# A four-layer graph network: the order of the attention's matmuls at the ends of a block, and the queues of the first loads

## Chip, cores and metric

The kernel runs on one core of a Trainium2 chip. The metric is the device time of one execution in microseconds. A core has these engines: PE (TensorE, matmuls), DVE (VectorE), ACT (ScalarE), POOL (GpSimd) and SP (SyncE, here only issuing transfers). Each works through its own queue of instructions in order; transfers are carried by 16 DMA engines.

## What is computed

x is 4096 x 256 in f32, adj a 4096 x 4096 matrix of 0 and 1 (about one entry in 128 is 1). Four layers follow one another; each takes h = relu(layernorm(x)) and adds its output to x. The change is in the attention of layers 0 and 2, cut to what matters:

```python
# layer 0 (h: 4096 x 256); its gating, which follows, is left out here
Wh = h @ W
e = Wh @ a_src + (Wh @ a_dst).T
e = jnp.where(e > 0, e, 0.2 * e)
e = jnp.where(adj > 0, e, jnp.float32(-9000000000000000.0))
h_attn = jax.nn.softmax(e, axis=1) @ Wh
...
# layer 2
h = x @ W
e = (h @ a[:D, 0])[:, None] + (h @ a[D:, 0])[None, :]
e = jnp.where(e > 0, e, 0.01 * e)
att_logits = jnp.where(adj > 0, e, -1e12)
return jax.nn.elu(jax.nn.softmax(att_logits, axis=1) @ h)
```

Layer 1 is a mean over neighbours, layer 3 an attention with queries and keys.

## The kernel before

**Stages.** By the trace, layer 0's projection and first loads take the first 76 us, its attention lasts to about 625 us, its dense part to 1230, layer 1 to 1530, layer 2's attention from there to 2018, layer 3 to the end.

**Attention in blocks.** `class Attention` (L192) serves layers 0 and 2. The 4096 rows are 32 tiles of 128. A block is a group of row tiles: in layer 0 two blocks of 2 tiles and seven of 4 (`cuts`, L453), in layer 2 eight of 4. For each block the columns are gone through in 16 pairs of column tiles (c, c + 1). In `run` (L338) a pair goes through four steps:

- `logits` (L325): DVE forms the logits of the pair in a buffer y (L332, one instruction for each of the two column tiles), POOL subtracts the mask from y (L336). There are 8 y buffers; a buffer is free again when the matmuls have read it.
- ACT takes the exponential of y (L363, two instructions).
- PE adds the pair to the block's accumulators (L374): for each row tile r one accumulator of 128 x 257 in PSUM, its first column the row sums of the exponentials. A pair of a block with 4 row tiles is 8 matmuls; in the trace an f32 matmul is two instructions, so 16.
- At a block's last pair, DVE inverts the row sums (`rden`, L382), and a finish function scales the accumulators out of PSUM: in layer 0 `finish0` (L442), even r on ACT (L449), odd r on DVE (L447), into xs; in layer 2 `finish2` (L920), even r on ACT (L930), odd on DVE (L926), into hp, with an exponential on ACT (L934) and two additions on DVE (L936, L937) behind it.

The program text runs the logits three pairs ahead of the matmuls (`LAG`). Layer 0 has 4 accumulator buffers (`att.run(es, LEAD, 4, ahead)`, L654), layer 2 has 5 (L1119). In the kernel before, the matmuls of a pair are written column tile by column tile, and for each over all r:

```python
for k in range(2):
    for r, acc in enumerate(accs[b]):
        nc.tensor.matmul(
            out=acc, lhsT=y[:, r, k, :], rhs=self.v[:, c + k, 0 : D + 1],
            start=(c + k == 0), stop=(c + k == NT - 1),
        )
```

**The maxima of the next block.** While a block is worked on, `reach` (L265) builds the running minimum for the next one on DVE (L278 for the first column tile, L280 for the others). At its end `top` (L286) copies it (ACT L291), transposes it (PE L294), reduces it (DVE L297 to L302) and transposes the result (PE, abT, L304), from which the rows for the next block's logits are spread over the partitions (PE L313 or two DMAs, L319 and L320).

**The mask.** In layer 0 `ahead` (L515) loads one adjacency tile after another (POOL's DMA, L486), transposes it on PE in 8 instructions (cT, L495), turns it into the mask on ACT (`turned`, L500) and stores it (codesT, SP, L520). Layer 2 loads the masks again with SP's DMAs.

**The beginning.** `load(1)` (L608) issues the first adjacency tile on POOL. SP then issues the eight DMAs of x, 512 KB each, and W, a_src and a_dst (`weights`, L219) between the first and second of them. `block0(b)` takes one x block at a time, staggered: statistics on DVE (L122, L123), the mean taken off on ACT, DVE and POOL (L629, L633), the power for the deviation on POOL (L117), for b = 0 the products of W with a_src and a_dst on DVE (`columns`, L242), further loads `load(2 * b + 6)` on POOL, the transposed masks of one unit, then transposes (L145) and the projection on PE (L154) with ACT's copies (L256), and two steps of `reach`.

**What sets the order.** The program text is written for all engines at once; a scheduler orders the instructions of each engine's queue from it and adds the waits. An engine does not overtake within its queue.

Of the kernel before, what the change touches and what calls it, by code (L numbers as in the profile page):

```python
# [41 lines left out]
def kernel(ctx: ExitStack, tc: tile.TileContext, w: dict, out: bass.AP):  # L42
    nc = tc.nc
    x, adj = w["x"], w["adj"]
    N, D = x.shape
    NT = N // P
# [64 lines left out]
    def rstd_of(pool, mv, n, tag, rs=None):  # L111

        ve = pool.tile([P, n], F32, tag=f"{tag}_ve", name=f"{tag}_ve")
        nc.vector.tensor_scalar(ve, mv[:, :, 1], EPS, None, ALU.add)
        if rs is None:
            rs = pool.tile([P, n], F32, tag=f"{tag}_rs", name=f"{tag}_rs")
        nc.gpsimd.tensor_tensor(rs, ve, mhalf[:, :n], ALU.pow)  # L117
        return rs

    def stats_of(pool, src, mv, tag):  # L120
        st = pool.tile([P, 6], F32, tag=f"{tag}_st", name=f"{tag}_st")
        nc.vector.bn_stats(st, src)  # L122
        nc.vector.bn_aggr(mv, st)  # L123
# [68 lines left out]
    class Attention:  # L192
# [145 lines left out]
        def run(self, es, lead, n_acc, ahead=lambda n: None):  # L338

            self.y_p = es.enter_context(tc.tile_pool(name=f"{self.tag}_y", bufs=self.n_y))  # L340
            self.ps_b = es.enter_context(
                tc.tile_pool(name=f"{self.tag}_b", bufs=1, space=PSUM)
            )
            ps_acc = es.enter_context(
                tc.tile_pool(name=f"{self.tag}_acc", bufs=n_acc, space=PSUM)
            )
            pairs = [(b, c) for b in range(len(self.blocks)) for c in range(0, NT, 2)]
            LAG = self.lag
            ys, accs = {}, {}
            for n in range(len(pairs) + LAG):  # L350
                if n < len(pairs):
                    b, c = pairs[n]
                    ahead(n)
                    if n + PPB + lead < len(pairs):
                        self.reach(n + PPB + lead)
                    y = self.y_p.tile([P, RB, 2, P], F32, tag="y", name="y")
                    ys[n] = y = y[:, 0 : self.blocks[b]["n"], :, :]
                    self.logits(y, b, c, self.turned(b, c // QT))
                if n >= LAG:
                    b, c = pairs[n - LAG]  # L360
                    y = ys.pop(n - LAG)
                    for k in range(2):
                        nc.scalar.activation(  # L363
                            y[:, :, k, :], y[:, :, k, :], AF.Exp,
                            bias=self.sdst[:, c + k : c + k + 1],
                        )
                    if c == 0:
                        accs[b] = [
                            ps_acc.tile([P, D + 1], F32, tag="acc", name="acc")
                            for _ in range(self.blocks[b]["n"])  # L370
                        ]
                    for k in range(2):
                        for r, acc in enumerate(accs[b]):
                            nc.tensor.matmul(  # L374
                                out=acc, lhsT=y[:, r, k, :], rhs=self.v[:, c + k, 0 : D + 1],
                                start=(c + k == 0), stop=(c + k == NT - 1),
                            )
                    if c == NT - 2:
                        done = accs.pop(b)
                        rden = self.small.tile([P, RB], F32, tag="rden", name="rden")  # L380
                        for r, acc in enumerate(done):
                            nc.vector.reciprocal(rden[:, r : r + 1], acc[:, 0:1])  # L382
                        self.finish(self.blocks[b]["at"], done, rden)
# [46 lines left out]
    with ExitStack() as l0:  # L430
# [10 lines left out]
        with ExitStack() as es:  # L441
# [19 lines left out]
            att = Attention(es, "l0", 0.2, 3, 8, cuts, turned_of, finish0, ps_c)  # L461
# [19 lines left out]
            def load(up_to):  # L481
                for b, q, r in units[len(raw) : up_to]:
                    pool = first_p if len(raw) < FIRST else adj_p

                    raw.append(pool.tile([P, QW], BF16, tag="adj", name="adj_t"))
                    nc.gpsimd.dma_start(out=raw[-1], in_=adj[ts(b * RB + r, P), ts(q, QW)])  # L486

            def fresh(up_to):

                load(up_to)  # L490
                for g in range(made[0], up_to):
                    (b, q, r), a = units[g], raw[g]
                    ps = ps_c.tile([P, QW], BF16, tag="top", name="cT")
                    for i in range(QT):
                        nc.tensor.transpose(ps[:, ts(i, P)], a[:, ts(i, P)], identb)  # L495
                    if (b, q) not in turned:
                        pool = kept_p if (b * NQ + q) % 8 < KEPT else turned_p
                        turned[b, q] = pool.tile([P, RB, QT, P], BF16, tag="turned", name="turned")
                    ct = turned[b, q][:, r, :, :]
                    nc.scalar.activation(  # L500
                        ct.rearrange("p c i -> p (c i)"), ps, AF.Exp,
                        scale=math.log(UNIT / WIDE), bias=log_wide,
                    )
                made[0] = max(made[0], up_to)
# [95 lines left out]
            with ExitStack() as ps_:  # L600
                wp = ps_.enter_context(tc.tile_pool(name="l0_w0", bufs=1))
                work = ps_.enter_context(tc.tile_pool(name="l0_prep", bufs=2))
                small = ps_.enter_context(tc.tile_pool(name="l0_ps", bufs=4))
                pst = ps_.enter_context(tc.tile_pool(name="l0_pst", bufs=2, space=PSUM))
                psm = ps_.enter_context(tc.tile_pool(name="l0_psm", bufs=3, space=PSUM))
                first_p = ps_.enter_context(tc.tile_pool(name="l0_first", bufs=FIRST))

                load(1)  # L608
                for b in range(NB):
                    nc.sync.dma_start(  # L610
                        out=xs[:, ts(b, BT), :],
                        in_=x[ts(b, BW), :].rearrange("(t p) d -> p t d", p=P),
                    )
                    if b == 0:
                        att.weights(
                            wp, w["L0_gnn_W"], (w["L0_gnn_a_src"], w["L0_gnn_a_dst"]), nc.sync
                        )

                def block0(b):
                    xb = xs[:, ts(b, BT), :]  # L620
                    mv = small.tile([P, BT, 2], F32, tag="pl_mv", name="pl_mv")
                    for i in range(BT):
                        stats_of(small, xb[:, i, :], mv[:, i, :], "pl")


                    for i in range(BT):
                        mean = mv[:, i, 0:1]
                        if i == 0:
                            nc.scalar.activation(  # L629
                                xb[:, i, :], xb[:, i, :], AF.Identity, scale=-1.0, bias=mean  # L630
                            )
                        else:
                            (nc.gpsimd if i == BT - 1 else nc.vector).tensor_scalar(  # L633
                                xb[:, i, :], xb[:, i, :], mean, -1.0, ALU.subtract, ALU.mult
                            )
                    rs = rstd_of(small, mv, BT, "pl")
                    if b == 0:
                        att.columns(work)
                    load(2 * b + 6)
                    fresh(b + 1)  # L640
                    yield
                    hT = transposed_block(work, pst, xb, "hT", turned=True)
                    yield
                    att.project(b, hT, psm, rs)
                    yield
                    for n in range(2 * b, 2 * b + 2):
                        att.reach(n)

                run_staggered([block0(b) for b in range(NB)], 2)
                fresh(needed(PPB + FRESH - 1))  # L650
                for n in range(PPB, PPB + LEAD):
                    att.reach(n)
# [5 lines left out]
        wp = l0.enter_context(tc.tile_pool(name="l0_w", bufs=1))  # L658
# [467 lines left out]
    with ExitStack() as l3:  # L1126
# [4 lines left out]
        with ExitStack() as es:  # L1131
            wp = es.enter_context(tc.tile_pool(name="l3_w", bufs=1))
# [222 lines left out]
```

## Time and profile before

| what | value |
|---|---|
| median of 3 runs | 2989.58 us (2987.57 to 2996.24) |
| the profiled execution | 2990.5 us |
| span of its profile | 2988.7 us |
| mean granted PE clock in it | 0.989 |
| PE busy | 2866.0 us, 96% |
| DVE, ACT, POOL busy | 64%, 43%, 32% |

The span runs from the first to the last instruction of the profiled execution; the 1.8 us between it and that execution's time lie around it. The profile names each group of instructions by line and engine, with busy time, and, apart from it, the idle time just before its instructions with what ended that idle time. "DMA turned<-codesT" as the ending event is the landing of a mask tile loaded again. PEld is the load of the stationary operand, which runs beside PE.

### The profile page before, as it was taken

The numbers are of one execution on the slowest core, as the hardware profiler recorded it, in microseconds if no ns is written. First come the engines' busy times: TensorE is split into PE (matmuls) and PEld (weight loads), VectorE is DVE, ScalarE is ACT, GpSimd is POOL, SyncE is SP. The second block draws the span as 40 slices with busy tenths as digits, with TensorE's granted clock in tenths as the row PEclk, the third lists the DMA queues.
The fourth block names the chain that finished last, engine by engine and source line by source line (L and its number), as shares of the span: only waits on it lengthen the run. The fifth ranks groups of instructions, "written<-read, shape, count | busy, mean of one in ns | idle before, by whom it ended". The sixth has DMA issues, their size and how long they took to land.

```text
span 2988.7 us, 35212 instructions
## 1 busy us (share of the span) xinstructions
PE 2866.0 (96%) x13381; PEld 2335.5 (78%) x13381; DVE 1907.1 (64%) x3458; ACT 1279.1 (43%) x1963; POOL 947.8 (32%) x718
## 2 busy tenths in 40 slices
PE   7989999999999999899989999999999999999999
PEld 5778888866556665788878777888888888888888
DVE  5777777534555554477689888646766566566653
ACT  5666655459997323892264433433212112111211
POOL 4667665544444433220045555540000000000000
PEclk9999999999999999999999999999999999999999
DMA  5766665234553000595342122002111111111100
GB/s 131 201 146 145 128 139 133 71 58 70 80 79 65 8 8 8 136 248 164 113 170 87 68 78 78 29 11 68 58 51 47 37 34 62 39 34 62 34 8 8
DMA packets 109161, 238.62 MB, mean 80 GB/s; under 512 B 10736, under 2 KB 31200, under 8 KB 100288
## 3 DMA queue, kind: packets, MB, share of 16 engines
q1 hardware_dynamic: 71296, 167.26, 16.3%
q0 software_dynamic: 37696, 69.11, 14.9%
q8 instruction: 105, 1.72, 0.2%
q14 instruction: 64, 0.52, 0.1%
HBM read 265.63 MB, written 37.81 MB: 102 GB/s over the span
## 4 chain that ended last, share of the span: by engine, by line
PE 66%; ACT 9%; DVE 8%; issue 6%; POOL 6%; DMA 4%; SPq 0%; POOLq 0%; DVEq 0%; ACTq 0%
PE acc L374 18%; PE acc L1287 15%; PE s L154 15%; PE mm L154 8%; PE acc L1019 8%; POOL y L336 4%; ACT sign L180 4%; DVE y L332 2%; DVE run L280 2%; DMA turned<-codesT 1%; PE cT L495 1%; DMA a<-in_adj_dram 1%; PE q_ps L154 1%; ACT t L712 1%; DMA xs<-in_x_dram 1%
## 5 line engine op out<-in xcount | busy, mean ns | idle before, releaser
L374 PE MATMUL acc<-v,y 128*128 128x257 f32 x4096 | 930.8, 386 | 23.9 <-ACT hp L930 12.7
L374 PEld LDWEIGHTS acc<-v,y 128*128 128x128 f32 x4096 | 776.2, 192 | 137.0 <-ACT hp L930 17.0
L336 POOL TENSOR_TENSOR y<-y,turned 128x1024 f32<-128x1024 f32 (+1 forms) x272 | 545.3, 2015 | 320.2 <-DVE y L332 260.1
L363 ACT ACTIVATE y<-y,sdst 128x512 f32<-128x512 f32 (+1 forms) x544 | 350.5, 690 | 410.9 <-POOL y L336 410.7
L332 DVE SCALAR_TENSOR_TENSOR y<-ab_row,cdst,b 128x512 f32<-128x512 f32 (+1 forms) x544 | 371.0, 710 | 139.9 <-PE acc L374 124.1
L1287 PE MATMUL acc<-v,y 128*128 128x257 f32 x2048 | 454.5, 380 | 0.4 <-DVE rden L1295 0.4
L154 PE MATMUL s<-qT,hT 128*128 128x256 f32 x2048 | 445.2, 379 | 0.7 <-ACT qT L1235 0.7
L1280 ACT ACTIVATE y<-y 128x1024 f32<-128x1024 f32 x128 | 132.2, 1055 | 714.3 <-DVE y L1279 710.0
L154 PEld LDWEIGHTS s<-qT,hT 128*128 128x128 f32 x2048 | 389.0, 190 | 54.2 <-ACT qT L1235 1.4
L1287 PEld LDWEIGHTS acc<-v,y 128*128 128x128 f32 x2048 | 387.1, 190 | 55.9 <-issue 0.8
L180 ACT ACTIVATE sign<-a,limits 128x1024 bf16<-128x1024 bf16 x256 | 293.8, 1148 | 18.5 <-DMA a<-in_adj_dram 13.0
L1249 DVE SCALAR_TENSOR_TENSOR y<-code,s 128x512 f32<-128x512 bf16 x256 | 175.8, 687 | 100.7 <-PE s L154 100.5
L280 DVE SCALAR_TENSOR_TENSOR run<-turned,v,run 128x512 f32<-128x512 bf16 (+1 forms) x279 | 193.2, 692 | 31.8 <-ACT turned L500 22.7
L280 DVE SCALAR_TENSOR_TENSOR run<-turned,dst,run 128x512 f32<-128x512 bf16 x248 | 186.5, 752 | 24.5 <-DMA turned<-codesT 20.4
L1279 DVE TENSOR_TENSOR y<-y,top 128x1024 f32<-128x1024 f32 x128 | 146.2, 1215 | 43.0 <-PE top L1273 43.0
L1256 DVE TENSOR_TENSOR mx<-mx,y 128x512 f32<-128x512 f32 x224 | 154.8, 691 | 7.5
L500 ACT ACTIVATE turned<-cT,log_wide 128x1024 bf16<-128x1024 bf16 x128 | 139.2, 1105 | 29.9 <-PE cT L495 29.5
L173 POOL DMA_DIRECT2D a<-in_adj_dram x128 | 75.1, 588 | 198.4 <-ACT sign L180 144.8
L154 PE MATMUL mm<-kept 128*128 128x512 f32 x288 | 135.5, 610 | 2.4 <-ACT sz L807 1.4
L1019 PE MATMUL acc<-early,eq 128*128 128x512 f32 x512 | 128.8, 401 | 2.2 <-DVE early L421 1.9
L1019 PE MATMUL acc<-late,eq 128*128 128x512 f32 x512 | 122.6, 391 | 0.0
L1019 PEld LDWEIGHTS acc<-early,eq 128*128 128x128 f32 x512 | 97.0, 191 | 26.2 <-DVE early L421 2.1
(233 smaller groups left out, 3007.1 us busy)
## 6 DMA issues: line engine op xcount, KB each, us to landing
turned<-codesT SPq DMA_DIRECT2D x36, 1024.0 KB, 4.8
adj_t<-in_adj_dram POOLq DMA_DIRECT2D x128, 256.0 KB, 5.5
codesT<-turned SPq DMA_DIRECT2D x32, 1024.0 KB, 5.1
a<-in_adj_dram POOLq DMA_DIRECT2D x128, 256.0 KB, 4.7
code<-codesT SPq DMA_DIRECT2D x128, 256.0 KB, 5.5
code<-codesT SPq DMA_DIRECT2D x64, 512.0 KB, 8.1
ab_row<-l_ab_d SPq DMA_DIRECT2D x14, 512.0 KB, 5.6
xs<-in_x_dram SPq DMA_DIRECT2D x8, 512.0 KB, 12.5
```

What stands on the lines that cost most here:

```text
L154: nc.tensor.matmul(out=ps, lhsT=lhsT_of(k), rhs=rhs_of(k), start=(k == 0), stop=(k == n - 1))
L180: nc.scalar.activation(sign, self.came[g], AF.Sign, bias=limits[:, v : v + 1], accum_out=over[:, t, v, q : q + 1],)
L280: nc.vector.scalar_tensor_tensor(st["run"], code, dst, st["run"], ALU.subtract, ALU.min)
L332: nc.vector.scalar_tensor_tensor(y[:, :, k, :], st["ab"][:, 0, :, :], self.cdst[:, c + k : c + k + 1], st["b"], ALU.add, ALU.max,)
L336: nc.gpsimd.tensor_tensor(y, y, mask[:, :, c % QT : c % QT + 2, :], ALU.subtract)
L363: nc.scalar.activation(y[:, :, k, :], y[:, :, k, :], AF.Exp, bias=self.sdst[:, c + k : c + k + 1],)
L374: nc.tensor.matmul(out=acc, lhsT=y[:, r, k, :], rhs=self.v[:, c + k, 0 : D + 1], start=(c + k == 0), stop=(c + k == NT - 1),)
L1019: nc.tensor.matmul(out=acc, lhsT=eqs[c // (NT // 2)][:, ts(c % (NT // 2), P)], rhs=v1[c // BT][:, c % BT, :, :], start=(c == 0), stop=(c = ...
L1249: nc.vector.scalar_tensor_tensor(y[:, :, c : c + 2, :], st["code"][:, :, c : c + 2, :], -BIG / UNIT, ps, ALU.mult, ALU.add,)
L1256: nc.vector.tensor_tensor(mx, mx, y[:, :, c : c + 2, :], ALU.max)
L1279: nc.vector.tensor_tensor(part, part, top, ALU.subtract)
L1287: nc.tensor.matmul(out=accs[r], lhsT=st["y"][:, r, c, :], rhs=v3[:, c, :], start=(c == 0), stop=(c == NT - 1),)
```

## The change

It has two parts.

In `run`, the pairs of a block that are its last two, and in every block but the first its first two, are held back one at a time: when the second of the two is there, the matmuls of both are issued together, for r = 0 the four column tiles, then for r = 1, and so on. For all other pairs the order stays as it was. The number of matmuls, the buffers and the finish functions are unchanged. A y buffer is read to the end when the last row tile of its group has been added.

At the program's beginning the second adjacency tile is issued together with the first (`load(2)`), and W, a_src and a_dst are issued on ACT's queue before x's loop. SP issues x alone.

```diff
-            ys, accs = {}, {}
+            accs, held = {}, []
+            ys = {}
...
-                    for k in range(2):
-                        for r, acc in enumerate(accs[b]):
-                            nc.tensor.matmul(
-                                out=acc, lhsT=y[:, r, k, :], rhs=self.v[:, c + k, 0 : D + 1],
-                                start=(c + k == 0), stop=(c + k == NT - 1),
-                            )
+
+
+                    held.append((c, y))
+                    edge = NT - 2 - c < 4 or b > 0 and c < 4
+                    if edge and len(held) < 2:
+                        continue
+                    terms = [(r, c1 + k, y1) for r in range(len(accs[b]))
+                             for c1, y1 in held for k in range(2)]
+                    if not edge:
+                        terms.sort(key=lambda term: term[1])
+                    for r, j, y1 in terms:
+                        nc.tensor.matmul(
+                            out=accs[b][r], lhsT=y1[:, r, j % 2, :], rhs=self.v[:, j, 0 : D + 1],
+                            start=(j == 0), stop=(j == NT - 1),
+                        )
+                    held.clear()
                     if c == NT - 2:
...
-                load(1)
+                load(2)
+                att.weights(
+                    wp, w["L0_gnn_W"], (w["L0_gnn_a_src"], w["L0_gnn_a_dst"]), nc.scalar
+                )
                 for b in range(NB):
                     nc.sync.dma_start(
                         out=xs[:, ts(b, BT), :],
                         in_=x[ts(b, BW), :].rearrange("(t p) d -> p t d", p=P),
                     )
-                    if b == 0:
-                        att.weights(
-                            wp, w["L0_gnn_W"], (w["L0_gnn_a_src"], w["L0_gnn_a_dst"]), nc.sync
-                        )
```

## The prediction

> **What bounds the kernel now.** I read the page first: the engines' busy shares and the costliest groups (line, engine, operation; busy us, mean ns; idle time just before them and what ended most of it).
>
> ```profile
> PE 2866.0 (96%) x13381; PEld 2335.5 (78%) x13381; DVE 1907.1 (64%) x3458; ACT 1279.1 (43%) x1963; POOL 947.8 (32%) x718
> ...
> L374 PE MATMUL acc<-v,y 128*128 128x257 f32 x4096 | 930.8, 386 | 23.9 <-ACT hp L930 12.7
> ...
> L332 DVE SCALAR_TENSOR_TENSOR y<-ab_row,cdst,b 128x512 f32<-128x512 f32 (+1 forms) x544 | 371.0, 710 | 139.9 <-PE acc L374 124.1
> ```
>
> TensorE is the bound, and DVE waits 124.1 us for it (a y buffer comes free when the matmuls have read it). So only TensorE's own idle or slow time counts, and the attention's matmuls have 23.9 us of it. The waits of TensorE in layer 0's attention (172 to 625 us), then in layer 2 (1530 to 2018 us; total, times, longest):
>
> ```profile
> PE acc L374 <- ACT xs L449: 9.3, 6, 3.4
> PE abT L304 <- DVE ab L302: 7.8, 6, 1.4
> ```
> ```profile
> PE abT L304 <- DVE ab L302: 13.1, 7, 3.0
> PE acc L374 <- ACT hp L930: 12.7, 10, 3.0
> PE acc L374 <- issue: 1.9, 1, 1.9
> ```
>
> 9.3 + 12.7 = 22.0 us are waits for an accumulator to be emptied; the 1.9 is layer 2's first matmul, no block's end. One end of a block in the timeline (start, us, instruction, [idle before]):
>
> ```profile
> 1771.15 0.75 DVE L278 TENSOR_SCALAR run<-turned,dst 128x512 f32<-128x512 bf16 x1 [3.81 <-DMA turned<-codesT]
> ...
> 1775.37 0.16 DVE L382 RECIPROCAL rden<-acc 128x1 f32<-128x1 f32 x1
> 1775.57 0.57 ACT L930 ACTIVATE hp<-acc,minus,rden 128x256 f32<-128x256 f32 x1 [4.17 <-DVE rden L382]
> ...
> 1776.18 0.70 PE L374 MATMUL acc<-v,y 128*128 128x257 f32 x2 [2.99 <-ACT hp L930]
> ...
> 1777.75 0.55 ACT L930 ACTIVATE hp<-acc,minus,rden 128x256 f32<-128x256 f32 x1
> ```
>
> TensorE stops at 1773.2; DVE, late after a transfer, comes to the reciprocal at 1775.37; ACT empties r0 and TensorE starts. The clock beside such stalls (us; busy and instructions; granted clock; DMA share; GB/s):
>
> ```profile
> 508.70:512.10 3.40, 3.40 (x9) 0.51 0.30 118
> 512.10:515.50 3.40, 3.40 (x23) 1.00 1.00 318
> 1778.40:1781.80 3.40, 3.40 (x8) 0.50 0.00 0
> 1839.80:1846.60 6.80, 5.57 (x12) 0.50 0.08 10
> ```
>
> After three of the largest stalls (3.35 us ending at 508.44; 2.99 and 1.46 ending at 1776.18 and 1778.35; 2.57 ending at 1840.09) TensorE runs at half clock. The program's beginning, in the chain of waits (start, us, what):
>
> ```profile
> 9.53 24.00 DMA xs<-in_x_dram
> 33.55 0.43 DVE pl_st L122
> ```
>
> **What the Trainium skill says.** *Perfetto Trace Analysis*, "Matmuls": independent matmul groups should rotate through PSUM banks, so that emptying one overlaps the next group's matmuls. The trace shows what happens without enough overlap: 22.0 us. *TensorE: Matmul & The Clock Gate*, "What's actually happening": the clock halves after an idle window of about 3.4 us, and the windows run free of the kernel. Slow stretches of 3.40 and 6.80 us agree; that stalls of 2.57 to 3.35 us are enough is this trace's. *PSUM — Partial Sum Buffer*, "Engine vs sequencer instructions": queues of ScalarE, VectorE and GpSimd are strict FIFO; the reciprocal behind DVE's L278 agrees. *DMA: Bandwidth & Descriptors*, "Issuing engines are not separate DMA queues": transfers from all issuers interleave on the same 16 engines, only issue time is saved. Before the change x beside the adjacency tiles agrees: DVE takes up three successive x blocks of 0.52 MB at 20.46, 27.40 and 33.55 us, some 0.08 MB/us of x.
>
> **The sum, part by part.** *Grouped matmuls.* No instruction is added or removed: 4096 matmul instructions stay, two per matmul. In the timeline 43 of them take 9.48 us, 0.22 us each. Before, r0's last matmul stands 6 instructions from the block's end and its first of the next block follows at once: 6 x 0.22 = 1.3 us to read its row sum, invert it, scale it out. The same gap for r1, r2, r3. After, 32 instructions close a block and 32 open the next (all but the first of a layer), each accumulator's 8 together. Between the last of r0 and the first of the next r0 lie 24: 5.3 us, again alike for each r. Layer 2's fifth buffer adds 8 more, 1.8 us.
>
> What must fit in: reciprocal to matmul took 1775.37 to 1776.18, 0.8 us. Ahead of it on DVE at worst one pair of L332 (2 x 0.71) and one of L280 (2 x 0.75): 2.9. Sum 3.7, under 5.3. On DVE all the emptying is 4 reciprocals (0.16) and two scalings (0.48), 1.6 us; on ACT two of 0.46 to 0.57, with a pair of exponentials (2 x 0.69) between. They fit the stagger of 1.76 us per accumulator. In the built program's order DVE has r0's reciprocal behind the logits of pair 5 of the next block, then r1's with its scaling, r2's, and logits of pair 6; TensorE's matmuls stand as written. So I take all 22.0 us as gone. Bounds: not below 0; if DVE is held up by a transfer ahead of the reciprocal (longest such wait in layer 2: 5.0 us) the cover is exceeded by 5.0 + 0.8 - 5.3 = 0.5 us, a boundary.
>
> *Half clock after the stalls.* 9 instructions in 3.40 us where 15.5 fit: 1.4 us. 8 likewise: 1.65. 12 in 5.57 busy us where 25 fit: 2.9. Sum 6.0. Without the stall the window is not idle, so I take 6.0; bound 0 to 6.0, since a wait for abT can take the window's place: such a half-clock stretch stands at 1563.4 to 1566.8 us already.
>
> *What the groups hold up.* Both y buffers of a group come free about at its end, the first of them up to 3.5 us later than before. There are 8: two in the closing group leave six, so pairs 0 to 5 of the next block are filled when it ends, and TensorE has four beyond the opening group (14 us). Queued behind the waiting L332 of pair 6 (and again pair 8) on DVE are the reciprocals of later r's and the running minimum (L280), whose end releases abT (L304). After an opening group DVE owes two pairs of 2.9 us while TensorE takes 3.52 for one: 2.3 us behind, won back by 0.6 a pair, so gone in four pairs, about where abT's chain begins. In layer 0 a pair lasts 3.97 us with its transposes: more slack. In layer 2 DVE has little:
>
> ```profile
> 1594.00:1652.00 58.00, 55.32 (x257) 47.84 (x256) 53.43 (x81) 24.07 (x39) 33.93 (x16) 1.00 0.23 82
> ```
>
> (PE, PEld, DVE, ACT, POOL busy): 53.4 of 58. I put 0.5 us on each of the seven abT waits there, 3.5, rounded to 4; bounds 0 and 2.3 x 7 = 16. What is late next is thus abT (7.8 + 13.1 us stay in any case).
>
> *The first blocks of layer 0* (76 to 172 us) wait for ACT and for transfers; their reordered matmuls I cost at nothing. If that cover goes, one order against the other is worth under 1 us a boundary, two boundaries.
>
> *Queues at the beginning.* The same bytes move. W and both a leave SP's queue: SP issues x's eight back to back, some 0.5 us each earlier. ACT issues three (0.5 us each) while it has no other work before x's first block. POOL issues the second adjacency tile near 2.4 us instead of 9, in a stretch (2.4 to 6.8) where it idles; four tiles follow instead of five. For x: the x packets alone move 0.385 MB/us (8 to 13 us), beside tiles 0.08. A tile of 1.3 us in that early stretch costs x 0.5 MB, 6 us at the slow rate. Against it, DVE's first instruction is now the product of W and a_src (L242) instead of x's statistics, so block 0's chain, and with it POOL's next four tiles, comes about 1.2 to 1.7 us later, which gives x the same time alone: -6. So 0, bounds -5 and +6. What hides it wholly or not at all is x block 6 (33.55 us), whose projection is followed by a chain of five of 5 us on TensorE to 62 us.
>
> Sum: -22.0 - 6.0 + 4 + 0 = -24. The profiled execution took 2990.5 us (span 2988.7, 1.8 around it): 2966.5. It lies 0.9 above the median of the runs, 2989.58: 2965.6, say **2966**.
>
> **Rivals.**
> 1. *DVE takes the place.* Layer 0 gains 9.3 + 1.4 = 10.7, of layer 2's 12.7 + 4.6 half goes into abT waits: -10.7 - 8.6 = -19.3 at best, -10.7 at worst: 2970 to 2979. For it: 53.4 of 58 us, and transfers of up to 5.0 us in DVE's queue. Against: DVE waits 45.7 us for y in layer 2, so it is ahead mostly.
> 2. *Slower: y buffers.* If two freed at once leave fewer than two exponentiated pairs ready at the opening group (the point from which it decides), TensorE waits a pair, 3.5 us, at 13 boundaries: 46 - 28 = +18: 3007. For: L332's 124.1 us of waiting for TensorE; the buffers are what throttles DVE. Against: six pairs filled.
> 3. *Nothing.* Either the reciprocals wait as long in DVE's queue, or each microsecond reappears at abT: 2989.
> 4. *Beginning helps too*, or the abT waits shrink as TensorE no longer cools: 2952 to 2957.
>
> **Chances.** Likeliest (2957 to 2970) 0.56; rival 1 (2970 to 2979) 0.22; rival 4 0.09; rival 3 0.07; rival 2 0.06. A measurement of this kernel tells 0.3% (9 us) from no change, so faster means under 2980.6: 0.56 + 0.22 + 0.09 = 0.87; same 0.07; slower 0.06. The range 2954 to 2979 leaves out rivals 2 and 3 and the end of 4.
>
> **What would show it.** Right: L374's idle falls from 23.9 to about 2, no wait of it for L449 or L930 as they were; no half clock right after block ends; abT waits 21 to 25 us. Wrong: abT waits of 30 us and more with DVE behind (rival 1); L374 waiting for ACT's exponentials after a boundary (rival 2); first attention matmul moved from 76.3 us by more than 2 us (the beginning).

## The result and the profile after

| | before | changed kernel |
|---|---|---|
| median of 8 runs each | 2990.07 us | 2981.64 us (2975.03 to 2984.07) |
| ratio | | 0.9968, 95% interval 0.9957 to 0.9980 |
| span of the profile | 2988.7 | 2980.1 |
| first attention matmul | 76.3 | 77.7 |
| layer 0, first to last attention matmul | 550.2 | 539.7 |
| layer 2, first to last attention matmul | 485.2 | 485.2 |

The change gains 8.4 us, where 24 were forecast and 2954 was the lower, 2979 the upper end of the range. The two profiles name the place: layer 0 gained 10.5 us, layer 2 nothing. One execution of each says this only roughly. The first two blocks of layer 0 wait for the first loads, and the time from the first attention matmul to the third block's start varies from 91.8 to 94.8 us over all the kernels below. From the third block on, layer 0 lasts 454.5 to 455.6 us in the four kernels that group no pairs there and 447.6 to 450.4 in the eleven that group at both ends, so some 6 us of the gain recur in layer 0. Layer 2 lasts 485.2 us before, and 485.2 and 482.5 in two kernels with the same grouped order (the changed kernel and `edges`): a gain of 0 to 3 us.

The groups of the page after, by line (busy us, mean ns; idle before them and what ended it):

```profile
PE 2862.3 (96%) x13381; PEld 2336.7 (78%) x13381; DVE 1907.5 (64%) x3458; ACT 1280.1 (43%) x1963; POOL 952.4 (32%) x718
...
L384 PE MATMUL acc<-v,y 128*128 128x257 f32 x4096 | 922.1, 384 | 1.9 <-issue 1.9
```

The 22.0 us of waits for an accumulator are all gone; the 1.9 is layer 2's first matmul, as before. So that step of the forecast held. The waits of TensorE in the changed kernel, layer 0's attention (172 to 618 us), then layer 2's (1520 to 2009):

```profile
PE abT L304 <- DVE ab L302: 9.1, 6, 1.8
PE top L294 <- ACT run_sb L291: 2.8, 3, 2.0
```
```profile
PE abT L304 <- DVE ab L302: 28.1, 7, 8.7
PE acc L384 <- issue: 1.9, 1, 1.9
```

In layer 0 the waits for abT rose from 7.8 to 9.1 us, and 2.8 of waits for the running minimum's copy are new: 4.1 given back. In layer 2 abT waits rose from 13.1 to 28.1: 15.0 for 12.7 emptied. The clock, in stretches of TensorE (us; busy and instructions; granted clock; DMA share; GB/s):

```profile
1732.50:1739.30 6.80, 3.40 (x9) 0.50 0.01 3
1797.10:1803.90 6.80, 4.30 (x11) 0.52 0.00 1
1861.70:1868.50 6.80, 4.23 (x11) 0.54 0.00 1
508.00:515.00 7.00, 7.00 (x45) 1.00 0.36 139
```

The half clock after layer 0's stall at 508 us is gone (last line: the same stretch of the program's work, at full clock). In layer 2 it now stands at the three longest waits for abT (8.7, 5.8 and 6.2 us). In all, layer 2 has 17 us at half clock before and 24 after; with layer 0 both kernels have 41. Half clock after an idle engine agrees with what the forecast cites of *TensorE: Matmul & The Clock Gate*, "What's actually happening" (an idle window halves the clock): here it came after waits for accumulators and after waits for abT alike. The length of a wait did not decide alone. Layer 2's first wait for abT, 3.02 us, was followed by 3.4 us at half clock in the changed kernel; the same wait of 3.04 us in `reuse` (below) was not.

**Where abT's wait comes from.** DVE's waits in layer 2, before (1530 to 2018 us) and after (1520 to 2009):

```profile
DVE y L332 <- PE acc L374: 45.7, 33, 2.1
DVE run L280 <- DMA turned<-codesT: 20.4, 8, 5.0
...
DVE run L278 <- DMA turned<-codesT: 9.0, 3, 3.8
```
```profile
DVE y L332 <- PE acc L384: 36.8, 28, 2.1
DVE run L280 <- DMA turned<-codesT: 28.7, 11, 5.0
...
DVE run L278 <- DMA turned<-codesT: 9.2, 3, 4.4
```

DVE waited 29.4 us for mask tiles before and 37.9 after, and less for TensorE. One block shows how such a wait reaches TensorE. The timeline of the changed kernel before its longest wait for abT, engine by engine (POOL, SP's queue, DVE, TensorE):

```profile
1721.35 2.13 POOL L336 TENSOR_TENSOR y<-y,turned 128x1024 f32<-128x1024 f32 x1 [1.43 <-ACT y L364]
...
1723.51 0.32 SPq L923 DMA_DIRECT2D turned<-codesT  x1
...
1724.52 1.40 DVE L332 SCALAR_TENSOR_TENSOR y<-ab_row,cdst,b 128x512 f32<-128x512 f32 x2
1728.39 2.34 DVE L280 SCALAR_TENSOR_TENSOR run<-turned,dst,run 128x512 f32<-128x512 bf16 x3 [2.48 <-DMA turned<-codesT]
1730.64 0.74 DVE L332 SCALAR_TENSOR_TENSOR y<-ab_row,cdst,b 128x512 f32<-128x512 f32 x1
1731.30 0.68 DVE L297 TENSOR_REDUCE m<-top 128x4 f32<-128x512 f32 x1
...
1735.60 0.15 DVE L302 SCALAR_TENSOR_TENSOR ab<-v,m 128x4 f32<-128x4 f32 x1
...
1723.10 4.07 PE L384 MATMUL acc<-v,y 128*128 128x257 f32 x18
1735.90 0.37 PE L304 MATMUL abT<-ident,ab 128*8 128x128 f32 x1 [8.74 <-DVE ab L302]
```

POOL's L336 at 1721.35 is the last reader of a mask tile (pair 11 of the block). Its end lets SP issue the next tile's transfer into that buffer (1723.51). DVE has the running minimum of that tile, which belongs to the block after next, at the front of its queue, and stands still until the tile has landed (2.48 us). Behind it wait the logits of pair 14 and L297 to L302, on which abT and so all of TensorE depends. From the transfer's issue to abT it takes 12.4 us. The same chain in the kernel before:

```profile
1732.85 0.32 SPq L914 DMA_DIRECT2D turned<-codesT  x1
...
1737.68 2.34 DVE L280 SCALAR_TENSOR_TENSOR run<-turned,dst,run 128x512 f32<-128x512 bf16 x3 [0.42 <-DMA turned<-codesT]
...
1739.49 4.07 PE L374 MATMUL acc<-v,y 128*128 128x257 f32 x18
1745.19 0.27 PE L304 MATMUL abT<-ident,ab 128*8 128x128 f32 x1 [1.63 <-DVE ab L302]
```

It takes 12.3 us there too; only TensorE comes later, 10.7 us after the transfer's issue (1743.56) in place of 3.7 (1727.16). This suggests a loop of POOL, SP, transfer and DVE that limits layer 2 a second time; the experiments test it. The lengths of the blocks that start at 1640.8, 1698.4, 1765.0 and 1829.3 in the changed kernel, from first matmul to the next block's first, are 57.6, 66.6, 64.3 and 64.8 us; those of the kernel before, from 1650.3, were 61.4, 60.9, 64.3 and 64.6. The block without a long wait for abT gained 3.8 us, the next lost 5.7, and the two behind it are as long as they were.

### The profile page after: what moved, and what is told of

The parts are those of the page before. It is cut to its first block, busy times and chain, and to the rows that moved or that the text cites. A ratio compares the mean times of both kernels' runs of the same rounds, so it can differ in the third digit from the quotient of the medians.

```text
span 2980.1 us, 35216 instructions
## 1 busy us (share of the span) xinstructions
PE 2862.3 (96%) x13381; PEld 2336.7 (78%) x13381; DVE 1907.5 (64%) x3458; ACT 1280.1 (43%) x1963; POOL 952.4 (32%) x718
## 4 chain that ended last, share of the span: by engine, by line
PE 71%; ACT 8%; DVE 6%; issue 5%; POOL 5%; DMA 4%; SPq 0%; POOLq 0%; DVEq 0%; ACTq 0%
PE acc L384 21%; PE acc L1296 15%; PE s L154 15%; PE mm L154 8%; PE acc L1028 8%; ACT sign L180 4%; POOL y L336 2%; DVE run L280 2%; DVE y L332 1%; PE cT L506 1%; DMA turned<-codesT 1%; DMA a<-in_adj_dram 1%; DMA xs<-in_x_dram 1%; PE q_ps L154 1%; ACT turned L511 1%
## 5 line engine op out<-in xcount | busy, mean ns | idle before, releaser
L384 PE MATMUL acc<-v,y 128*128 128x257 f32 x4096 | 922.1, 384 | 1.9 <-issue 1.9
L384 PEld LDWEIGHTS acc<-v,y 128*128 128x128 f32 x4096 | 775.9, 192 | 109.7 <-issue 2.5
L336 POOL TENSOR_TENSOR y<-y,turned 128x1024 f32<-128x1024 f32 (+1 forms) x272 | 548.9, 2032 | 301.8 <-DVE y L332 222.4
L1296 PE MATMUL acc<-v,y 128*128 128x257 f32 x2048 | 454.5, 380 | 0.4 <-DVE rden L1304 0.4
L280 DVE SCALAR_TENSOR_TENSOR run<-turned,v,run 128x512 f32<-128x512 bf16 (+1 forms) x279 | 193.1, 692 | 26.5 <-ACT turned L511 17.1
L280 DVE SCALAR_TENSOR_TENSOR run<-turned,dst,run 128x512 f32<-128x512 bf16 x248 | 186.5, 752 | 32.5 <-DMA turned<-codesT 28.7
## 6 DMA issues: line engine op xcount, KB each, us to landing
xs<-in_x_dram SPq DMA_DIRECT2D x8, 512.0 KB, 21.5
```

The lines of the kernel that those rows point to most:

```text
L280: nc.vector.scalar_tensor_tensor(st["run"], code, dst, st["run"], ALU.subtract, ALU.min)
L336: nc.gpsimd.tensor_tensor(y, y, mask[:, :, c % QT : c % QT + 2, :], ALU.subtract)
L384: nc.tensor.matmul(out=accs[b][r], lhsT=y1[:, r, j % 2, :], rhs=self.v[:, j, 0 : D + 1], start=(j == 0), stop=(j == NT - 1),)
L1296: nc.tensor.matmul(out=accs[r], lhsT=st["y"][:, r, c, :], rhs=v3[:, c, :], start=(c == 0), stop=(c == NT - 1),)
```

## The experiments

The theory formed from this, A: layer 2 has a second bound, DVE standing at the running minimum for a transfer that could only just be issued. Its rivals: B, the gain was lost elsewhere; B2, the y buffers that a group holds cost it; C, DVE's own work sets the 64 us. Each ratio below is to the kernel before, run beside it (medians 2988.87 to 2989.80 us); the time of a layer comes from one profile of each kernel.

**Each part of the change alone.** `edges` has the matmuls' change and the old beginning, `start` the reverse; `l0only` is `edges` with the grouping in layer 0 alone:

```diff
-                    edge = NT - 2 - c < 4 or b > 0 and c < 4
+                    edge = self.tag == "l0" and (NT - 2 - c < 4 or b > 0 and c < 4)
```

> The grouped matmuls alone, the program's beginning as before. The trace of the changed kernel has its first attention matmul at 77.74 us, before it was at 76.31, so I expect the new queues to have cost 1.4 us: 2980.2 us, ratio 0.9967, first attention matmul near 76.3. If the 1.4 us is the noise of one execution, or is made up again in the first two blocks, the time is that of the changed kernel, 2981.6.

Measured: 2980.95 us, ratio 0.9969 (0.9959 to 0.9979), first attention matmul at 74.1.

> The new queues alone, matmuls as before. If they cost 1.4 us: 2991.5 us, ratio 1.0005, first attention matmul near 77.7. If they cost nothing: 2990.1. In no case do they hide 15 us of the gain that is missing.

Measured: 2988.62, ratio 0.9997 (0.9988 to 1.0007), first attention matmul at 75.3. The 1.4 us was one execution's: the new queues are worth nothing that can be measured. The four kernels with the new beginning started their attention anywhere from 72.7 (`opening`, below) to 77.7 us (the changed kernel), those with the old one from 74.1 to 79.5.

> Grouped matmuls in layer 0 alone, beginning and layer 2 as before. Theory A (layer 2 has a second bound, the loop of mask transfers, running minimum and logits on DVE, so that its 12.7 us of emptied stalls come back as waits for abT): layer 0 gives its 10.5 us, layer 2 lasts 485 us either way: 2979.6, ratio 0.9965, the same as the grouped matmuls in both layers. Theory B (grouping helps in layer 2 as well, what was lost was lost elsewhere): slower than grouping in both layers by up to 12.7 us: 2990 to 2992.

Measured: 2981.83, ratio 0.9975 (0.9965 to 0.9985); layer 2 lasted 484.8 us with the old order, 482.5 in `edges` with the new. B's 2990 is out: what the change brings, layer 0 brings, but for at most some 3 us.

**The transfers taken away.** `reuse` is `edges` with the masks of the first two blocks used again for the later ones; `reuse_before` is the kernel before with the same edit. Both leave out 24 of layer 2's 32 mask transfers and so do not compute layer 2.

```diff
     def stored(b, q):
+        b = b % 2
```

> Grouped matmuls, beginning as before, and layer 2 takes for every block the masks of the first two blocks, which stay where they are: 24 of its 32 mask transfers are left out. Theory A (DVE stands at the running minimum until a transfer has landed that could only be issued when POOL gave a buffer free, with the next logits behind it): blocks of 64 to 66 us become blocks of 57.5, layer 2 goes from 485 to about 463 us, total 2958, abT waits in layer 2 from 28 to under 13. Theory C (the buffers y held by a group, or DVE's own work of 51 to 54 us a block, set the 64 us): the transfers are hidden anyway, under 5 us gained: 2975 to 2980.

Measured: 2959.88, ratio 0.9895 (0.9879 to 0.9912). Layer 2 lasted 461.0 us, where A said 463, with abT waits of 11.8 us and full clock throughout the layer:

```profile
PE abT L304 <- DVE ab L302: 11.8, 7, 3.0
```

C is out, and so is B2 as the cause: with both groups' y buffers held as before, DVE does the same 367 us of work in 461 us as in 485:

```profile
1522.35:2007.50 485.15, 457.10 (x2085) 396.96 (x2086) 367.47 (x588) 199.15 (x307) 277.50 (x134) 0.98 0.18 62
```
```profile
1524.48:1985.46 460.98, 449.15 (x2085) 391.41 (x2086) 366.99 (x588) 198.93 (x307) 276.86 (x134) 1.00 0.03 11
```

(layer 2 in the changed kernel, then in `reuse`; busy us of PE, PEld, DVE, ACT, POOL; clock; DMA share; GB/s.) The edit does more than take transfers away: the scheduler, too, then puts the running minima of the later blocks still further ahead on DVE, the last block's by six pairs, and abT a few matmuls earlier in one or two blocks. `follow2` below moves the running minima the other way, keeps every transfer, and gains as well; what it has in common with `reuse` is that DVE no longer stands waiting for a transfer.

> The kernel before, with layer 2 reusing the masks of its first two blocks: 24 of 32 mask transfers left out, matmuls in the old order. Theory A (two bounds in layer 2: the stalls at block ends on TensorE, and the loop of transfers and DVE): with the loop gone the old stalls at block ends remain, shortened where a transfer had delayed the reciprocal; layer 2 lasts 485 - 12 = 473 us, total 2978; against the grouped matmuls without transfers (2959.9) 18 us, of which 10.5 are layer 0's and some 8 layer 2's. Theory D (block ends only stall because of the transfers, so grouping is worth nothing in layer 2 at all): 461 + 2 us in layer 2, total 2968.

Measured: 2969.85, ratio 0.9934 (0.9922 to 0.9946); layer 2 467.0 us, its waits for accumulators 4.1 in place of 12.7 us, its abT waits 11.9. That is between A and D: two thirds of the stalls at block ends go with the transfers, and grouping is worth 467.0 - 461.0 = 6.0 us here. The loop costs the kernel before 485.2 - 467.0 = 18.2 us, and the grouped one 482.5 - 461.0 = 21.5. Both expectations missed, on either side.

**Half of the grouping.** Both on the changed kernel with its new beginning, `closing` groups only the last two pairs of a block, `opening` only the first two:

```diff
-                    edge = NT - 2 - c < 4 or b > 0 and c < 4
+                    edge = NT - 2 - c < 4
```
```diff
-                    edge = NT - 2 - c < 4 or b > 0 and c < 4
+                    edge = b > 0 and c < 4
```

> As the changed kernel, but only the last two pairs of a block are grouped; the first two are added column tile by column tile. r0 to r2 still have 24 to 12 instructions to be emptied in, r3 only 6 (1.3 us). Theory A: layer 0 gives back some 0.5 us a block (3 of its 10.5), layer 2 stays at 482 to 485, since what TensorE saves there comes back at abT: 2983. Theory B2 (the y buffers that the opening group holds bring DVE behind): layer 2 gains 8 us and more: 2974.

Measured: 2980.05, ratio 0.9968 (0.9956 to 0.9980); layer 0 542.1, layer 2 480.4 us. As fast as with both groups: the closing group alone brings as much. From its third block on, layer 0 lasted 449.3 us, as with both groups, so it gives nothing back. Layer 2 is 2 to 5 us shorter than with both groups (482.5 and 485.2), which is short of B2's 8 us; the two profiles with both groups already differ by 2.7.

> As the changed kernel, but only the first two pairs of a block are grouped. r0 has 6 instructions (1.3 us) to be emptied in, r1 to r3 12 to 24. The stall at the first accumulator stays in layer 0 (0.8 to 3.4 us at six block ends), the second ones in layer 2 go. Layer 0: as before, 549 us; layer 2: 482 to 485, as in every kernel with the transfers just in time. Total 2987 to 2990. If opening groups alone empty the path: 2981.

Measured: 2983.50, ratio 0.9981 (0.9973 to 0.9989); layer 0 552.4, layer 2 479.7 us. The total missed its 2987 to 2990. In layer 0, 5.7 of the 9.3 us of stalls stayed, while waits for abT and the running minimum's copy rose from 7.8 to 13.4 us; from its third block on it took 457.9 us, some 3 more than without groups. Layer 2 was 2 to 5 us better than expected, which the runs don't explain.

**Smaller mask tiles.** If the loop costs, perhaps smaller steps of it cost less. `half` has 16 buffers of 512 KB, `quarter` 32 of 256 KB, both on `edges` (the main part of the edit; PART is half or a quarter of QT, and the readers' indices follow it):

```diff
-            loaded[b, q] = turned_p.tile([P, RB, QT, P], BF16, tag="turned", name="turned")
-            nc.sync.dma_start(out=loaded[b, q], in_=codesT[b][q])
+            loaded[b, q] = turned_p.tile([P, RB, PART, P], BF16, tag="turned", name="turned")
+            at = q * PART
+            nc.sync.dma_start(
+                out=loaded[b, q], in_=codesT[b][at // QT][:, :, at % QT : at % QT + PART, :]
+            )
```

> Grouped matmuls, beginning as before, and layer 2's masks in 16 buffers of half the size, so that a half is given free, and loaded anew, two pairs earlier or follows two pairs later. All work is done. Theory A: the transfer lands two pairs (5 to 7 us) earlier against the logits for the first half of a tile, the waits of DVE for transfers (37 us with grouped matmuls) fall by half, layer 2 goes from 482 to 460 to 472 us: 2960 to 2971. Theory C (DVE's own work sets the 64 us a block): as with whole tiles, 2981.

Measured: 2976.91, ratio 0.9962 (0.9950 to 0.9975); layer 2 479.2 us, DVE's waits for transfers still 25.5 us.

> As the kernel with half tiles, but 32 buffers of a quarter: 256 KB each, four times as many transfers. Theory A: no slower than with halves unless SP's queue (where the two transfers of abT stand among them) holds them back: 2958 to 2970. If small transfers cost DVE more waits instead: 2975 or more.

Measured: 2997.63, ratio 1.0024 (1.0016 to 1.0033), layer 2 498.7 us, DVE's waits for transfers 40.6 us (`edges`: 37.0). Both missed. `half` is not clearly faster than `edges` (their intervals overlap). The transfers of these sizes took 3.8 and 3.0 us from issue to landing where whole tiles took 4.8: a quarter of the bytes in 0.6 of the time. And the scheduler moved DVE's order along. A buffer comes free behind pair 3 of a block with whole tiles, pair 1 with halves and pair 0 with quarters; in layer 2's later blocks the first running minimum of the next use stands behind the logits of pair 5, 3 and 2. So DVE comes to it too early again. That points to the place in DVE's queue rather than the tile's size; why `quarter` lost as much as it did is not shown.

**DVE's order.** In the built programs of before and after alike, from layer 2's fourth block on, DVE has the first running minimum of the block after next behind the logits of pair 5 of a block, while its transfer starts when POOL is done with pair 3. The following edit, on `edges`, binds the running minimum behind the logits of three pairs earlier, in layer 2 alone (`follow2`; `follow4` has 4 in place of 2 at both places, so five pairs earlier; `follow2_before` is the kernel before with the edit of `follow2`). Two lines that keep DVE's last instruction at hand are left out:

```diff
                     if n + PPB + lead < len(pairs):
-                        self.reach(n + PPB + lead)
+                        if self.tag == "l2" and n > 2:
+                            with tc.issue_after(after[n - 1 - 2]):
+                                self.reach(n + PPB + lead)
+                        else:
+                            self.reach(n + PPB + lead)
...
+                    after[n] = self.last.ins
```

> Grouped matmuls, beginning as before, and in layer 2 the running minimum of a pair is queued on DVE behind the logits of three pairs earlier, where the scheduler had put it some five pairs further ahead. All work is done and every transfer is made; only DVE's order differs: the first running minimum of the block after next stands behind pair 10 of a block in place of pair 5, while its mask transfer is still free to start when POOL has finished pair 3. Theory A (DVE stood at a running minimum that nobody needed yet, with logits behind it): DVE's waits for transfers fall from 37 us to under 8, layer 2 from 482 to 461 to 465 us, as where the transfers were left out: total 2960 to 2963. Theory C (too much traffic or work): 2975 or more. A risk: DVE has less to do while it waits for a y buffer, and comes late with abT; then abT waits of 20 us, 2970.

Measured: 2969.84, ratio 0.9929 (0.9916 to 0.9941). Transfers no longer hold DVE: in layer 2 it waits for none, where it waited 37.9 us. But layer 2 took 472.8 us: the risk that was named. The abT waits, and what DVE waits for instead, the next block's rows through ACT's copy b (4.9 us in the changed kernel):

```profile
PE abT L304 <- DVE ab L302: 16.8, 6, 3.6
```
```profile
DVE y L332 <- ACT b L330: 29.6, 6, 6.8
```

> As with three pairs, but the running minimum may stand five pairs ahead (first of a block behind pair 7). Theory A: transfers, issued behind pair 3, have landed by then as well: 2960 to 2965. If the slack is too small, the waits come back in part: 2970.

Measured: 2969.94, ratio 0.9935 (0.9922 to 0.9947), layer 2 470.6 us, abT waits 16.4.

> The kernel before with DVE's order of layer 2 alone changed as above, matmuls not grouped. Theory A: as the kernel before without the transfers (layer 2 467 us, total 2970): 2970, some 20 us faster than before; grouping on top of it is worth 10 us. If DVE's order only pays with grouped matmuls: 2985.

Measured: 2973.70, ratio 0.9942 (0.9929 to 0.9956), layer 2 470.5 us. So DVE's order alone, with the matmuls untouched, is worth about twice the change. And with this order grouping brings layer 2 nothing again (472.8 against 470.5): waits for accumulators were only 3.2 us, and abT waits are 16.8 against 11.1.

> DVE's order of layer 2 as in the kernel with five pairs of lead, matmuls grouped in layer 0 alone. If grouping is worth nothing in layer 2 even where no transfer holds DVE (abT takes the stalls' place): layer 0 as with grouping, layer 2 470 us: 2967 to 2970, the same as with both layers grouped (2969.9). If grouping still helps there: 2974 to 2976.

Measured: 2966.09, ratio 0.9917 (0.9900 to 0.9933), layer 2 466.5 us. Grouped in layer 2 as well it was 470.6 (abT waits 9.7 against 16.4). That grouping costs 4 us there is not shown: the scheduler also put the first running minimum behind pair 9 in three of the four later blocks, where `follow4` has it behind pair 7, and the intervals of the two ratios overlap.

**abT later in TensorE's queue.** The last two kernels make two changes at once: they bind the running minimum behind the logits of seven pairs earlier, and begin it three pairs ahead in place of five, so that the scheduler puts abT two pairs later on TensorE. `lead3h6` groups in both layers, `l0lead3h6` in layer 0 alone. The second change:

```diff
-            for n in range(PPB, PPB + LEAD):
+            for n in range(PPB, PPB + 3):
                 att2.reach(n)
...
-        att2.run(es, LEAD, 5)
+        att2.run(es, 3, 5)
```

> Matmuls grouped in both layers, DVE's running minimum in layer 2 bound behind the logits of seven pairs earlier, and given three pairs ahead in place of five: by the built order the transposes of the maxima then stand at pair 9 of TensorE in place of 7, abT at pair 10 in place of 8, and DVE's reduction behind the last logits of a block (pair 15) in place of between pairs 13 and 14. If the abT waits (16.4 us, and the 6.7 us of lost clock after them) are what ends last: they fall under 8 us, layer 2 goes from 471 to 460 us, 2959. If the rows then come too late for the next block's logits and TensorE waits for exponentials: 2970 or more.

Measured: 2951.61, ratio 0.9866 (0.9847 to 0.9885). Layer 2 lasted 454.2 us, 31 less than before; the clock was full throughout.

```profile
PE abT L304 <- DVE ab L302: 5.2, 6, 1.3
```
```profile
1522.36:1976.60 454.24, 449.00 (x2085) 391.46 (x2086) 356.26 (x592) 197.76 (x307) 273.89 (x134) 1.00 0.18 66
```

TensorE is busy for 449.0 of 454.2 us, with all the transfers made (66 GB/s). It is the fastest of all the kernels, 7 us better than the 2959 expected. What each of the two changes is worth alone was not measured.

> As the run before, with the matmuls of layer 2 in the old order. If grouping is worth what it emptied in layer 2 once neither transfers nor abT hold TensorE (6 us between the two kernels that left the transfers out): 2965, 6 us slower than with both layers grouped. If not: the same time.

Measured: 2961.34, ratio 0.9902 (0.9887 to 0.9918); layer 2 460.5 us, waits for accumulators back at 8.4 us, abT 0.5.

```profile
PE acc L390 <- ACT hp L946: 8.4, 13, 1.8
```

Here grouping is worth 460.5 - 454.2 = 6.3 us in layer 2, as between the two kernels without transfers (6.0), and the medians differ by 9.7.

## Why the forecast was wrong

**The emptied stalls: right.** 22.0 us forecast, 22.0 gone. The 5.3 us between an accumulator's last and first matmul covered the emptying at every block end, even where DVE waited 4.4 us for a mask tile just ahead of the reciprocal (at 1698.12 us).

**The half clock: wrong in layer 2, and in part luck in layer 0.** Layer 2's stretches moved to the waits for abT, which the forecast had as its bound of 0 ("a wait for abT can take the window's place"). Layer 0's stretch went in the changed kernel, but in six of the eleven kernels that group there at both ends one of 3.4 us stands at 528 to 533 us instead, behind the new wait of some 2 us for the running minimum's copy.

**What the groups hold up: the step that failed.** It put "0.5 us on each of the seven abT waits there, 3.5, rounded to 4", with 16 as the upper end; measured were 15.0 us in layer 2 and 4.1 in layer 0, 19.1 for 4. The mechanism it argued (DVE behind by held y buffers, won back by 0.6 us a pair) was the wrong one: without transfers abT waits are 11.8 us with the groups (`reuse`) and 11.9 without (`reuse_before`). The working took DVE to be free between its instructions (53.4 busy of 58 us, in a block without a wait for a mask tile) and counted the waits for mask tiles only as a delay of the reciprocal. But DVE cannot win back time across those waits: each tile's transfer starts from POOL's last use of a buffer, which follows DVE's own logits, and takes 4.8 us. When TensorE is quicker, it merely comes to abT earlier. In the block that began at 1711.70 us before and at 1698.35 after, the logits of pair 6 began 7.7 us ahead of TensorE's second pair before, and 1.2 us behind it after. *PSUM — Partial Sum Buffer*, "Engine vs sequencer instructions" (strict FIFO), was cited for the reciprocal; the same rule at the L280 of another block was what decided: the 2.48 us wait above had logits queued behind it, and `follow2`, which moves the running minimum back, has no such wait.

**The rivals.** Rival 1, a place taken by DVE through transfers in its queue, was the right one, and too small: it left layer 2 half of its gain, which kept little or nothing, so 2981.64 lies above its 2979 too. It was given 0.22. Its sign came: abT waits of 37.2 us with DVE behind, where 30 was the limit. The argument against it, that DVE "is ahead mostly", read 45.7 us of waits for TensorE as slack in every block. But 32.9 of them lie in the last two blocks, where no running minimum is left to build. In the block from 1711.70 us DVE is busy for 49.4 of 60.9 us, and waits:

```profile
DVE run L280 <- DMA turned<-codesT: 5.3, 2, 4.9
DVE run L278 <- DMA turned<-codesT: 3.8, 1, 3.8
DVE y L332 <- PE acc L374: 1.1, 1, 1.1
```

Rival 2 (TensorE starved of pairs at the opening) did not come: no wait of L384 for an exponential.

**The beginning: right.** 0 forecast, ratio 0.9997 for `start`. Single profiles differ by more than the effect.

**The sum as measured**, from the two profiles. By time: first attention matmul +1.4 (chance), layer 0's attention -10.5, layer 2's 0.0, rest +0.5: -8.6 of span, -8.4 in the medians. By the forecast's terms: the stalls -22.0, what took their place +19.1. What is left of the -8.6 is mostly the first two blocks of layer 0, -2.5, which is within chance, and TensorE's busy time, -2.7 in the rest of layer 0 and -2.4 in layer 2. The -2.4 is not the clock's: where no half clock stands in layer 2, its busy time differs in the same way, 451.0 us in `reuse_before` and 449.2 in `reuse`, 451.6 in `l0lead3h6` and 449.0 in `lead3h6`. It goes with the grouped order; the forecast had no such term.

What stays open: why the grouped order keeps TensorE busy for some 2 us less (the profile models where a matmul ends); why `opening` and `closing` had a slightly quicker layer 2 than both groups together; which of the two last changes did how much; and how near 454 us layer 2 can come to its 449 of TensorE work.

## What to carry to other kernels

A stall taken off the busiest engine is a gain only until the next chain that paces it, so measure that chain before pricing the stall: leave out its transfers, or look how long it takes from its first release (here a buffer given free) to the engine that waits, and how far ahead of that engine it runs. Work that is queued far ahead of its need on an engine that keeps its order is not free filler when it waits for a transfer: everything behind it waits too. Here it was cheaper to queue it later (-16 us for an order of DVE alone) than to speed up what it holds (at most some -4 with half tiles). And once the second chain is out of the way, try the first change again: grouping was worth 0 to 3 us in layer 2 at first, nothing with DVE's order alone, and 6 us once abT came later as well.

## What was not expected of the hardware

Mask tiles of 1024, 512 and 256 KB took 4.8, 3.8 and 3.0 us from issue to landing: a quarter of the bytes took 1.8 us less, and the kernel with such tiles was 17 us slower (`quarter` against `edges`). Beginnings that are the same in every instruction reach their first attention matmul up to 5 us apart (72.7 to 77.7 us), so effects of a few microseconds there can't be read from one profile. Waits of TensorE of the same length, 3.02 and 3.04 us, at the same place of the program were followed by half clock in one kernel and not in the other.
